# A fused two-layer graph attention on one core: step 1's first hidden tile turned by VectorE and sixteen transfers instead of TensorE

## The chip, the core and the metric

The kernel runs on one core of a Trainium2 chip. The metric is the device time of one execution in microseconds (us). The kernel before took 3073.7 us (median of three runs, 3072.74 to 3074.0).

Six instruction streams matter here. TensorE (PE; its weight loads are listed apart as PEld) multiplies and can also transpose a 128x128 tile. VectorE (DVE), ScalarE (ACT) and GpSimd (POOL) do the elementwise work. SyncE (SP) issues nearly all the transfers (DMA). Each stream runs its instructions in order, so an instruction that waits holds up whatever stands behind it on its own stream.

## What is computed

The input x is 64 graphs of 256 nodes with 512 features; adj is a boolean 256x256 adjacency per graph. Two layers are applied, each to a normalised and rectified copy of x, and each is added back:

```python
# layer 0
h = jnp.maximum(_layernorm(x, axis=-1), 0.0)
x = x + _L0_gnn_ref(h, adj, ...)      # 4 heads of 64, masked softmax attention over the 256 nodes, then Wo, bo
# layer 1
h = jnp.maximum(_layernorm(x, axis=-1), 0.0)
x = x + _L1_gnn_ref(h, adj, ...)      # layernorm with gamma, beta; 8 heads of 64; mask with the diagonal added; then w_out, b_out
```

All tiles are float32, apart from the masks.

## The kernel before

Two graphs form a step (G = 2, so 512 rows, in four row tiles t = 0 to 3 of 128 rows), and there are 32 steps. The steps are software-pipelined: while TensorE works on layer 1 of step s, the other engines prepare layer 0 of steps s+1 and s+2. The order of the work is written out by hand. Each call `at(period, place, function, ...)` puts a function at a place on a line of abstract time; at the end all calls are sorted by place and run, and this emits the instructions. Inside one engine they stay in that order. "Place" is therefore an order, not a time.

The matrix products use a seven-product scheme on 2x2 blocks (`PRODUCT`, the tuples `SET`, `SETC`), for which GpSimd builds sums of the weights (`weight_sum`, L410) and of the activations (`act_sums0`, `act_sums1`, L413 to L418). `project_qk` (L902) computes the queries and keys this way; its first product of a set needs only the block B0 of the turned activations `hT`, and its second (product 6) needs a sum, B4.

A product needs h with the features on the partitions, which is `hT`. There are two ways to get there:

- By TensorE. `transpose_h` (L735) does 16 transposes into PSUM, and ScalarE rectifies them out of PSUM into `hT` (L739). The function `by_tensor` says for which step and layer this is done: step 0 and, for layer 0, step 1, and for layer 1 the last step.
- By VectorE and transfers. `turn_blocks` (L759) transposes the 32x32 blocks of one row tile; `move_blocks` (L771) then carries the blocks to their partitions with sixteen transfers of 64 KB from SP; `place_h` (L782) rectifies them into `hT` on ScalarE. All the other steps do it so.

Step 0 has nothing to hide behind, so its front is special. `norm0` computes a row tile's mean and variance on VectorE (L647, L648, L676) and the inverse root on GpSimd (L677); `first_scale` (L688 on VectorE, L689 on ScalarE) scales it; `first_turn` (L798) transposes it on TensorE; `first_fill` rectifies the first graph (g = 0) and the second (g = 1) into `hT`, the even feature chunks on ScalarE (L809) and the odd on VectorE (L807); `first_qk` (L820) projects. For step 1 `norm0` computes all four tiles and `row_scales` (L657 to L659, GpSimd) and `scale_row` (L663, ScalarE) follow.

All early loads stand on SP's queue in this order: x of step 0 and Wq, Wk, Wv in halves, x of step 1 (L512), two of the eight transfers of w_qkv's first two blocks (L481), the adjacency of step 1 (L517), the other six, w_out (L478), Wo in two halves (L453), the two biases (L458), the third block of w_qkv, and later x of step 0 once more for the residual (`load_x`, L524). The program's list of waits has eight semaphores for SP's transfers, used in turn, so that each transfer also waits until the one eight places before it has landed.

The weights of layer 1 are turned on the way: `weight_turn` (L490) on VectorE for w_qkv, `weight_block` (L498 on TensorE, L500 out of PSUM on ScalarE) for w_out. `mask_scores` (L1078) adds the mask on VectorE, `exponentials` (L1083) are on ScalarE, `weigh` (L1126) multiplies with the values, `weigh_out` (L1141) copies the result out, `normalise` (L1202, GpSimd) divides by the sums, and for step 0 `combine_rows` (L1025) applies Wo.

Two limits of memory matter as well: PSUM has four banks for scores and four for everything else, and a product that takes a bank waits for the copy that empties it.

Of the kernel before, what the change touches and what calls it, by code (L numbers as in the profile page):

```python
# [8 lines left out]
FP = mybir.dt.float32  # L9
# [3 lines left out]
AF = mybir.ActivationFunctionType  # L13
# [305 lines left out]
def fast_path(  # L319
# [21 lines left out]
    nc = tc.nc  # L341
    P = 128
    B, N, D = x.shape
    DH = 64
    G = 2
    NSTEP = B // G
    NIC = N // P
    NT = G * NIC
    T = G * N
    NC = D // P  # L350
# [7 lines left out]
    act = ctx.enter_context(tc.tile_pool(name="act", bufs=1))  # L358
# [40 lines left out]
    Q, NQ = 32, P // 32  # L399
# [12 lines left out]
    def act_sums0(b, eng=nc.gpsimd):  # L412
        eng.tensor_tensor(b[:, 3], b[:, 5], b[:, 0], ALU.subtract)  # L413

    def act_sums1(b, eng=nc.gpsimd):
        eng.tensor_tensor(b[:, 4], b[:, 2], b[:, 3], ALU.subtract)
        eng.tensor_tensor(b[:, 5], b[:, 2], b[:, 5], ALU.subtract)
        eng.tensor_tensor(b[:, 6], b[:, 1], b[:, 4], ALU.subtract)  # L418


    H0, H1, HD = I0 // 2, I1 // 2, D // 2
# [3 lines left out]
    wo0 = const.tile([P, NB, HP0, HD], FP, name="wo0")  # L425
# [23 lines left out]
            )  # L449

    def later_weights():
        for i in range(2):
            nc.sync.dma_start(  # L453
                wo0[:, 2 * i:2 * i + 2].rearrange("p j c o -> p (j c) o"),
                wo[:, i * HD:(i + 1) * HD].rearrange("(c p) o -> p c o", p=P),
            )
        for v, t in ((bo, bo_b), (b_out, bout_b)):
            nc.sync.dma_start(t, bass.AP(tensor=v.tensor, offset=v.offset, ap=[[0, P], [1, D]]))  # L458

# [13 lines left out]
    def weight_load(n):  # L473

        pool, tag = ((act, "v1"), (io, "xt"), (act, "v1"), (act, "turned"))[n]
        wr = pool.tile([P, 4, D], FP, name="wr", tag=tag)
        if n == 3:
            nc.sync.dma_start(wr, w_out.rearrange("(r p) i -> p r i", p=P))  # L478
        else:
            for b in range(NQ):  # L480
                nc.sync.dma_start(  # L481
                    wr[b * Q:(b + 1) * Q].rearrange("p r i -> p (r i)").rearrange("p (r i) -> p r i", i=P),
                    w_qkv[n * D:(n + 1) * D, b * P:(b + 1) * P].rearrange("(r p) i -> p r i", p=Q),
                )
        return wr
# [199 lines left out]
    def first_scale(t):  # L685
        st = S[0]
        r, mr = st["r"][:, t:t + 1], st["mr"][:, t:t + 1]
        nc.vector.tensor_scalar(mr, st["mean"][:, t, 0:1], r, -1.0, op0=ALU.mult, op1=ALU.mult)  # L688
        nc.scalar.activation(st["h"][:, t, :], st["h"][:, t, :], AF.Identity, bias=mr, scale=r)  # L689

# [55 lines left out]

    def by_tensor(s, lyr):

        return s == 0 or s == (1, NSTEP - 1)[lyr]


    def turn_blocks(s, lyr, t):

        st = S[s]
        if "blocks" not in st:
            st["blocks"] = act.tile([P, NQ, NC, NT, Q], FP, name="blocks", tag=("turned", "h")[lyr])
        nc.vector.transpose(  # L759
            st["blocks"][:, :, :, t, :].rearrange("p b c n -> p c b n"),  # L760
            st["h"][:, t, :].rearrange("p (c b n) -> p c b n", c=NC, b=NQ),
        )
# [39 lines left out]
    def first_fill(g):  # L802
        for c in range(NC):
            b0, _, step = B_OF[c // HC]
            dst, src = S[0]["hT"][:, b0 + g * step, c % HC, :], S[0]["ph"][c][:, g]
            if c % 2:
                nc.vector.tensor_scalar(dst, src, 0.0, None, op0=ALU.max)  # L807
            else:
                nc.scalar.activation(dst, src, AF.Relu)  # L809

    def first_qk(g, i):

        st = S[0]
        if g == 0:
            st["qk", 0, i] = sm.tile([P, 2, T], FP, name="qk", bufs=2)
        bank = mm_tile([P, 2, N])
        terms = [(k, j, c) for k in range(2) for j in range(2) for c in range(HC)]
        for k, j, c in terms:
            b0, _, step = B_OF[j]
            nc.tensor.matmul(  # L820
                bank[:, k, :], wqk0[:, A_OF[i, j], c, k, :], st["hT"][:, b0 + g * step, c, :],
                start=(k, j, c) == terms[0], stop=(k, j, c) == terms[-1], skip_group_check=True,
            )

        def rest():
            cols = slice(g * N, (g + 1) * N)
            nc.vector.tensor_tensor(st["qk", 0, i][:, 0, cols], bank[:, 0, :], st["ne"][:, cols], ALU.mult)
            nc.scalar.copy(st["qk", 0, i][:, 1, cols], bank[:, 1, :])
        return rest
# [382 lines left out]
    def at(period, place, fn, *args):  # L1212
        events.append((period * (PERIOD if period >= 0 else FIRST) + place, len(events), fn, args))
# [7 lines left out]
    def at_set(period, place, order, fn, *args):  # L1221
        for i, n in enumerate(order):
            at_dense(period, place + i / 7, 1 / 7, fn, *args, n)
# [58 lines left out]
    AT_X, AT_C0, AT_QK, AT_Q0, AT_V0, AT_H1, AT_Z = 2.0, 3.0, 3.5, 4.5, 5.5, 6.06, 6.2  # L1282
# [8 lines left out]
    p = NSTEP - 2  # L1291
# [15 lines left out]
    for s in range(NSTEP):  # L1307

        p = s - 2
# [8 lines left out]
        else:  # L1318
            at(p - 1, 4.9, adjacency_pack, s)
        for t in range(NT):  # L1320
            at(p, ((0.5, 0.9, 1.73, 1.74)[t], (1.6995, 1.6996, 2.0295, 2.0296)[t], -6.3 + 0.01 * t)[s] if s < 3 else (0.95, 1.05, 1.2, 1.35)[t], norm0, s, t)
            if s == 0:
                at(p, (0.95, 1.35, 1.745, 2.15)[t], first_scale, t)
            else:
                at(p, (2.375 + 0.001 * t, (-5.8, -5.799, -5.6, -5.599)[t])[s - 1] if s < 3 else 1.6 + 0.001 * t, scale_row, s, t)
            if not by_tensor(s, 0):
                at(p, AT_X - 0.00035 + 0.00001 * t if s > 2 else (2.6, 2.601, 2.72, 2.721)[t], turn_blocks, s, 0, t)
        if not by_tensor(s, 0):
            at(p, AT_X - 0.00031 if s > 2 else 3.0, move_blocks, s)
        for g in range(G):  # L1330
            if s < 3:
                at(p, (1.8, 2.03, -5.8)[s] + 0.001 * g, neighbours, s, g)
            else:
                at(p - 1, AT_Q0 - 0.0009, neighbours, s, g)
        if s < 2:
# [5 lines left out]
        for a in range(NQ if s > 2 else 0):  # L1341
            place = AT_X - 0.00031 if a > 2 else 1 + (a + 4) / 7 - 0.0005
# [4 lines left out]
        if s == 0:  # L1347
            at(p - 1, 5.72, warm)
            for t in range(NT):
                at(p, (1.0, 1.4, 3.31, 3.32)[t], first_turn, t)  # L1350
            for g in range(G):
                at(p, (1.72, 3.33)[g], first_fill, g)
                for i in range(2):
                    rest = []
                    place, end = ((3.0, 3.5), (3.64, 3.969), (3.97, 4.299), (4.3, 4.638))[g * 2 + i]
                    at(p, place, lambda g=g, i=i, rest=rest: rest.append(first_qk(g, i)))
                    at(p, end, lambda rest=rest: rest[0]())
        else:
            for c in range(NC):
                if by_tensor(s, 0):  # L1360
                    at(p, 2.9292 + 0.0001 * c, transpose_h, s, 0, c)
                else:
                    at(p, AT_Q0 - 0.001 + 0.0001 * c, place_h, s, 0, c)
            at(p, AT_Q0 - 0.0005 if s > 1 else FIRST_C0 + 0.1, lambda s=s: act_sums0(S[s]["hT"]))
            at(p, AT_Q0 - 0.0004 if s > 1 else FIRST_C0 + 0.101, lambda s=s: act_sums1(S[s]["hT"]))
            at_set(p, 3.3 if s < 2 else AT_Q0, SET, project_qk, s, 0, 0)
        if s < 2:
            for t in range(NT):
                place = (FIRST_V0 + 0.14 * t - (0 if t else 0.0005), (4.31, 5.02, 5.16, 5.31)[t])[s]
# [7 lines left out]
        p = s - 1  # L1377
# [20 lines left out]
        for k in range(NT):  # L1398
# [6 lines left out]
            place = ((3.6112, 3.6113, 3.7502, 3.7503)[k], 3.6 + 0.01 * k, AT_Q0 + (-0.0002, -0.00019, 0.0002, 0.00021)[k])[edge]  # L1405
# [11 lines left out]
        p = s  # L1417
        if s < NSTEP - 1:
# [3 lines left out]
            p, place = (s + 1, 1.0) if s < NSTEP - 2 else (s, LAST_QK + 2)  # L1422
# [5 lines left out]
        else:  # L1428
            p = s - 1
# [43 lines left out]
    gbr, blocks = [], {}  # L1473
    at(-3, 5.7, first_loads)
    at(-3, 5.705, lambda: gbr.append(first_gamma()))
    at(-2, 4.93, later_weights)
    for i in range(4):
        at(-2, 4.301 if i else FIRST_Q0 + 0.32, weight_sum, nc.gpsimd, wqk0, i)
        at(-1, 1.21, weight_sum, nc.gpsimd, wo0, i)
    for n, place in ((0, 4.0), (1, 4.0), (3, 4.0), (2, 5.0)):  # L1480
        at(-2, place, lambda n=n: blocks.update({n: weight_load(n)}))
    at(-2, FIRST_V0 + 0.2, lambda: gamma_beta(gbr[0]))
    for i in range(12):
        place = (
            4.6395, 4.6396, 4.9, 4.901, 4.902, 5.19965, 5.19966, 5.7, 12.6, 12.601, 12.602, 13.0,
        )[i]
# [55 lines left out]
```

## Time and profile before

| | |
|---|---|
| median of three runs | 3073.7 us (3072.74 to 3074.0) |
| the profiled execution: its time, and the span of its profile | 3072.65 us, 3070.9 us |
| busy, of the span: PE, DVE, POOL, ACT | 3063.4, 2534.3, 2295.8, 1212.2 us |
| PE busy from 15 to 3000 us | 2984.96 of 2985 us |
| granted TensorE clock | 1.00 up to 3000 us, 0.98 in the last 71 us |
| DMA share in 5 to 10, 15 to 20, 20 to 25, 30 to 35, 50 to 55 us | 1.12, 1.26, 1.23, 0.89, 0.16 |
| the 16 transposes of step 1 for layer 0 (L735) on the chain of waits | 34.27 us, for 1.75 us |

A timeline row has the start in us from the start of the span, the time it covers, the engine (SPq and ACTq are transfers being issued), the line, the operation, the tile written and the tiles read, the shape, and in square brackets the idle time in front of it with what ended it. In a view of groups, the last numbers are busy time and the mean of one in ns. The DMA share is the mean busy share of the 16 DMA engines; packets that wait in a queue count, so it can pass 1.

### The profile page before, as it was taken

The page shows a single profiled execution, that of the slowest core. Times are in us where ns is not written, and L with a number is a line of the kernel's source. Part 1 is how long each engine was busy: PE and PEld are TensorE (multiplying, and loading weights), DVE is VectorE, ACT ScalarE, POOL GpSimd, SP SyncE. Part 2 cuts the span into 40 slices and gives each one's busy share as a digit, 9 for nine tenths or more (in the row PEclk, how much of TensorE's full clock was granted, in tenths as well). Part 3 has the DMA queues.
Part 4 walks back from the last instruction along what each step waited for, and adds up shares of the span by engine and source line. Part 5 has one row for each costly group of instructions (what it writes and reads, how often), then busy time and mean ns, then how long its engine had stood idle before and what let it go on. Part 6 is the DMA issues. An engine that isn't in the chain of part 4 may idle for free.

```text
span 3070.9 us, 55407 instructions
## 1 busy us (share of the span) xinstructions
PE 3063.4 (100%) x20106; PEld 2527.4 (82%) x20106; DVE 2534.3 (83%) x4739; ACT 1212.2 (39%) x2133; POOL 2295.8 (75%) x2120
## 2 busy tenths in 40 slices
PE   9999999999999999999999999999999999999999
PEld 7888888888888888888888888888888888888887
DVE  7888888888888888888888888888888888888766
ACT  5443443434343343433444333443434344343431
POOL 6877787777877777777877777787777877778753
PEclk9999999999999999999999999999999999999999
DMA  6223222233222331323323233222232222332311
GB/s 159 58 88 95 78 75 85 74 95 95 60 88 71 100 95 53 91 73 94 95 60 90 74 89 94 75 77 80 81 94 83 72 83 74 101 91 56 92 35 50
DMA packets 192365, 251.20 MB, mean 82 GB/s; under 512 B 58264, under 2 KB 84504, under 8 KB 192088
## 3 DMA queue, kind: packets, MB, share of 16 engines
q1 hardware_dynamic: 128800, 180.46, 20.8%
q10 hardware_dynamic: 63288, 67.15, 7.5%
q8 instruction: 161, 2.64, 0.4%
q14 instruction: 116, 0.95, 0.1%
HBM read 128.59 MB, written 34.34 MB: 53 GB/s over the span
## 4 chain that ended last, share of the span: by engine, by line
PE 100%; DVE 0%; issue 0%; ACT 0%; POOL 0%; POOLq 0%
PE mm L902 38%; PE mm L999 19%; PE mm L983 13%; PE sc L1055 9%; PE sc L1126 6%; PE mm L949 6%; PE mm L1126 5%; PE mm L1055 3%; PE mm L932 1%; PE mm L1025 0%; PE mm L820 0%; PE mm L789 0%; PE mm L735 0%; PE mm L498 0%; PE sc L798 0%; PE mm L553 0%
## 5 line engine op out<-in xcount | busy, mean ns | idle before, releaser
L902 PE MATMUL mm<-hT,wqkv 128*128 128x256 f32 x3584 | 787.4, 380 | 0.0
L902 PEld LDWEIGHTS mm<-hT,wqkv 128*128 128x128 f32 x3584 | 677.9, 190 | 102.6 <-issue 11.4
L1090 POOL TENSOR_TENSOR pd<-p 128x512 f32<-128x512 f32 x383 | 480.1, 1275 | 253.4 <-ACT p L1083 195.5
L999 PE MATMUL mm<-wo,oT 128*128 128x256 f32 x2632 | 578.8, 379 | 0.0
L999 PEld LDWEIGHTS mm<-wo,oT 128*128 128x128 f32 x2632 | 499.7, 190 | 69.2 <-issue 0.7
L1083 ACT ACTIVATE p<-p 128x512 f32<-128x512 f32 x766 | 441.4, 627 | 102.8 <-DVE p L1078 91.1
L1078 DVE TENSOR_TENSOR p<-sc,n 128x512 f32<-128x512 f32 x579 | 363.1, 683 | 113.1 <-PE sc L1055 113.1
L983 PE MATMUL mm<-wqkv,hT 128*128 128x256 f32 x1792 | 395.2, 381 | 0.0
L902 PE MATMUL mm<-hT,wqk 128*128 128x256 f32 x1736 | 383.7, 381 | 0.0
L983 PEld LDWEIGHTS mm<-wqkv,hT 128*128 128x128 f32 x1792 | 337.9, 190 | 55.0 <-issue 10.3
L902 PEld LDWEIGHTS mm<-hT,wqk 128*128 128x128 f32 x1736 | 327.0, 190 | 53.5 <-issue 10.3
L870 POOL TENSOR_TENSOR xt<-xt,u 128x512 f32<-128x512 f32 x183 | 233.1, 1274 | 140.3 <-DVE xt L864 67.4
L1055 PE MATMUL sc<-qk 64*128 64x256 f32 x2320 | 292.7, 385 | 0.0
L1055 PEld LDWEIGHTS sc<-qk 64*128 64x128 f32 x2320 | 217.8, 186 | 59.7 <-issue 27.6
L1096 DVE STREAM_TRANSPOSE turned_p<-pd 128x1024 f32<-128x1024 f32 x192 | 237.2, 1235 | 26.6 <-POOL pd L1090 25.9
L663 ACT ACTIVATE h<-h,mr,r 128x512 f32<-128x512 f32 x252 | 187.9, 806 | 170.0 <-POOL mr L659 170.0
L1202 POOL TENSOR_TENSOR oT<-oT 128x512 f32<-128x512 f32 x188 | 240.2, 1278 | 1.1 <-DMA oT<-line 1.1
L1103 DVE TENSOR_REDUCE part<-turned_p 128x32 f32<-128x1024 f32 x192 | 233.2, 1215 | 4.4
L1126 PE MATMUL sc<-p,v 128*32 128x256 f32 x3152 | 190.8, 382 | 0.0
L949 PE MATMUL mm<-hT,wv 128*128 128x256 f32 x840 | 188.3, 382 | 0.0
L855 ACT COPY u<-mm 128x512 f32<-128x512 f32 x62 | 36.4, 586 | 368.9 <-PE mm L999 221.7
L949 PEld LDWEIGHTS mm<-hT,wv 128*128 128x128 f32 x840 | 156.6, 190 | 26.8 <-ACT vT L836 6.2
(162 smaller groups left out, 4443.9 us busy)
## 6 DMA issues: line engine op xcount, KB each, us to landing
h<-blocks SPq DMA_DIRECT2D x960, 64.0 KB, 2.0
oT<-line SPq DMA_DIRECT2D x376, 128.0 KB, 3.0
h<-in_x_dram SPq DMA_DIRECT2D x31, 1024.0 KB, 5.6
xt<-in_x_dram ACTq DMA_DIRECT2D x60, 512.0 KB, 4.8
out_dram<-xt SPq DMA_DIRECT2D x32, 512.0 KB, 3.1
v<-values ACTq DMA_DIRECT2D x480, 32.0 KB, 1.9
out_dram<-xt ACTq DMA_DIRECT2D x30, 512.0 KB, 4.4
ne<-ne SPq DMA_DIRECT2D x90, 64.0 KB, 2.0
```

Source lines behind the costliest of these rows:

```text
L902: nc.tensor.matmul(bank[:, k, :], w[:, wa, c, k, a * P:(a + 1) * P], st["hT"][:, ba, c, :], start=first and (k, c) == (0, 0), stop=(k, c) ...
L949: nc.tensor.matmul(bank, wv0[:, wa, c, :], st["hT"][:, ba, c, :], start=first and c == 0, stop=c == HC - 1, skip_group_check=True,)
L983: nc.tensor.matmul(bank[:, t, :], st["hT"][:, ba, c, t * P:(t + 1) * P], wqkv1[:, wa, c, 2, :], start=first and (t, c) == (0, 0), stop=(t, ...
L999: nc.tensor.matmul(bank[:, t, :], oT[:, ba, c, t * P:(t + 1) * P], w[:, wa, c, :], start=first and (t, c) == (0, 0), stop=(t, c) == (NIC - ...
L1055: nc.tensor.matmul(sc[g][e][:, kc, :], qk[rows, 1, k0:k0 + P], qk[rows, 0, g * N:(g + 1) * N], start=True, stop=True,)
L1078: nc.vector.tensor_tensor(p[e][:, g], sc[e], neg[:, :, g, :], ALU.add)
L1083: nc.scalar.activation(p[e][:, g], p[e][:, g], AF.Exp, scale=SCALE)
L1090: nc.gpsimd.tensor_tensor(st["pd"][:, e], p[e][:, :, 0, :], p[e][:, :, 1, :], ALU.add)
L1096: nc.vector.transpose(st["turned_p"], st.pop("pd").rearrange("p e g (b k) -> p (e g b) k", k=32))
L1103: nc.vector.tensor_reduce(st["part", lyr, prs][:, i], st.pop("turned_p"), axis=mybir.AxisListType.X, op=ALU.add)
L1126: nc.tensor.matmul(po[r0:r0 + 32, g, :], (st["v1"][:, g * NIC + kc, pr * P + r0:pr * P + r0 + Q] if lyr else st["v0"][:, r0 // Q, pr, g * ...
L1202: nc.gpsimd.tensor_tensor(dst, dst, invb, ALU.mult)
```

## The change

Six things change, all in the first 50 us of the program. From there on the order of each engine's work is the same as before.

1. `by_tensor` no longer holds for step 1 of layer 0: its `transpose_h` is replaced by `turn_blocks`, `move_blocks` and `place_h`. The `blocks` tile takes the buffer with the tag "h".
2. `norm0` of step 1 moves up in front of the second and third result of `first_qk` on VectorE, `row_scales` on GpSimd in front of the masks of step 0, and `scale_row` on ScalarE in front of the third copy of `first_qk`. The neighbour maxima of step 1 (`neighbours`, L587) move behind the turns.
3. `first_fill` of graph 0 is done by ScalarE alone, and VectorE does the odd chunks of graph 1 only.
4. `first_scale` of row tile 1 is cut into two halves of 256 columns; for row tile 3 its VectorE part moves in between the two neighbour maxima of step 0.
5. The load of w_out moves in front of w_qkv's first block on SP's queue.
6. Wo is loaded by one transfer instead of two.

On SP's queue the sixteen new transfers stand behind the eight of w_qkv and in front of Wo, the two biases, the third block of w_qkv, the first line of sums (L1173) and `load_x`. The buffers change with the order: `load_x` of step 0 now takes the buffer that holds w_qkv's second block until its last `weight_turn`, where it took the buffer of step 1's h before; and the last of the four score banks of step 0's second pair of heads is one that `mask_scores` has to empty first, where it was one that `weigh_out` had to empty.

```diff
     def later_weights():
-        for i in range(2):
-            nc.sync.dma_start(
-                wo0[:, 2 * i:2 * i + 2].rearrange("p j c o -> p (j c) o"),
-                wo[:, i * HD:(i + 1) * HD].rearrange("(c p) o -> p c o", p=P),
-            )
+        nc.sync.dma_start(
+            wo0[:, :4].rearrange("p (i j) c o -> p i (j c) o", i=2), wo.rearrange("(c p) (i o) -> p i c o", p=P, i=2)
+        )
...
-        nc.scalar.activation(st["h"][:, t, :], st["h"][:, t, :], AF.Identity, bias=mr, scale=r)
+        for cols in (slice(0, D // 2), slice(D // 2, D)) if t == 1 else (slice(0, D),):
+            nc.scalar.activation(st["h"][:, t, cols], st["h"][:, t, cols], AF.Identity, bias=mr, scale=r)
...
-        return s == 0 or s == (1, NSTEP - 1)[lyr]
+        return s == 0 or (s, lyr) == (NSTEP - 1, 1)
...
-            st["blocks"] = act.tile([P, NQ, NC, NT, Q], FP, name="blocks", tag=("turned", "h")[lyr])
+            st["blocks"] = act.tile([P, NQ, NC, NT, Q], FP, name="blocks", tag="h" if lyr or s == 1 else "turned")
...
-            if c % 2:
+            if g and c % 2:
                 nc.vector.tensor_scalar(dst, src, 0.0, None, op0=ALU.max)
...
-            at(p, ((0.5, 0.9, 1.73, 1.74)[t], (1.6995, 1.6996, 2.0295, 2.0296)[t], -6.3 + 0.01 * t)[s] if s < 3 else (0.95, 1.05, 1.2, 1.35)[t], norm0, s, t)
+            at(p, ((0.5, 0.9, 1.73, 1.74)[t], 1.231 + 0.001 * t, -6.3 + 0.01 * t)[s] if s < 3 else (0.95, 1.05, 1.2, 1.35)[t], norm0, s, t)
             if s == 0:
-                at(p, (0.95, 1.35, 1.745, 2.15)[t], first_scale, t)
+                at(p, (0.95, 1.35, 1.745, 1.80005)[t], first_scale, t)
             else:
-                at(p, (2.375 + 0.001 * t, (-5.8, -5.799, -5.6, -5.599)[t])[s - 1] if s < 3 else 1.6 + 0.001 * t, scale_row, s, t)
+                at(p, (1.7 + 0.001 * t, (-5.8, -5.799, -5.6, -5.599)[t])[s - 1] if s < 3 else 1.6 + 0.001 * t, scale_row, s, t)
             if not by_tensor(s, 0):
-                at(p, AT_X - 0.00035 + 0.00001 * t if s > 2 else (2.6, 2.601, 2.72, 2.721)[t], turn_blocks, s, 0, t)
+                at(p, AT_X - 0.00035 + 0.00001 * t if s > 2 else 2.0295 + 0.0001 * t if s == 1 else (2.6, 2.601, 2.72, 2.721)[t], turn_blocks, s, 0, t)
         if not by_tensor(s, 0):
-            at(p, AT_X - 0.00031 if s > 2 else 3.0, move_blocks, s)
+            at(p, AT_X - 0.00031 if s > 2 else (2.03, 3.0)[s - 1], move_blocks, s)
         for g in range(G):
             if s < 3:
-                at(p, (1.8, 2.03, -5.8)[s] + 0.001 * g, neighbours, s, g)
+                at(p, (1.8, 2.3685, -5.8)[s] + 0.0001 * g, neighbours, s, g)
...
-                    at(p, AT_Q0 - 0.001 + 0.0001 * c, place_h, s, 0, c)
+                    at(p, (AT_Q0 - 0.001 if s > 1 else 2.9292) + 0.0001 * c, place_h, s, 0, c)
...
-    for n, place in ((0, 4.0), (1, 4.0), (3, 4.0), (2, 5.0)):
+    for n, place in ((3, 3.1), (0, 4.0), (1, 4.0), (2, 5.0)):
         at(-2, place, lambda n=n: blocks.update({n: weight_load(n)}))
```

## The prediction

> **What bounds the kernel now.** I read the page first, then the chain of waits of the first 62 us, then that stretch's timeline with the DMA issues, because the change touches nothing later.
>
> ```profile
> span 3070.9 us, 55407 instructions
> PE 3063.4 (100%) x20106; PEld 2527.4 (82%) x20106; DVE 2534.3 (83%) x4739; ACT 1212.2 (39%) x2133; POOL 2295.8 (75%) x2120
> ```
>
> TensorE works all the time. Work taken from it is therefore gained in full, and every new stop of it is lost in full: with PE busy 2984.96 of 2985 us from 15 us on, there is no idle time later that could swallow either. At most 7.5 us of idle exist, 1.39 at the start (for the identity) and most of the rest in the last 71 us. The chain around the transposes:
>
> ```profile
> 30.62 3.65 PE mm L932 x16
> 34.27 1.75 PE mm L735 x16
> 36.02 1.86 PE sc L1126 x32
> 37.88 1.93 PE sc L1055 x16
> 39.81 1.92 PE mm L902 x8
> 41.73 0.44 PE mm L498 x4
> ```
>
> The 16 transposes take 1.75 us, and TensorE does not stop in front of them or behind them. What stands on the other engines at that moment:
>
> ```profile
> 34.74 2.07 ACT L739 ACTIVATE hT<-mm 128x512 f32<-128x512 f32 x4
> 37.51 1.28 DVE L490 STREAM_TRANSPOSE wqkv<-wr 128x512 f32<-128x512 f32 x2
> 37.95 0.59 ACT L1141 COPY oT<-sc 128x512 f32<-128x512 f32 x1 [1.14 <-PE sc L1126]
> 38.43 1.28 ACT L612 ACTIVATE rows<-identb,any_of 128x128 bf16<-128x128 bf16 x4
> 38.98 2.48 DVE L1078 TENSOR_TENSOR p<-sc,n 128x512 f32<-128x512 f32 x4 [0.19 <-PE sc L1055]
> 39.70 2.43 ACT L1083 ACTIVATE p<-p 128x512 f32<-128x512 f32 x4
> 42.50 0.65 ACT L500 COPY wo<-mm 128x256 f32<-128x256 f32 x2
> 44.18 0.61 PE L498 MATMUL mm<-ident,wr 128*128 128x128 f32 x4
> ```
>
> ScalarE has 1.14 us of idle here and VectorE 0.19. Neither has much in reserve if something comes late. The last row is TensorE's second `weight_block`; it needs the bank that the ACT copies at 42.50 empty, and it stands 1.03 us behind them. And the transfers:
>
> ```profile
> 12.74 8.54 SPq L481 DMA_DIRECT2D wr<-in_L_gnn_w_qkv_dram  x6
> 21.33 1.26 SPq L478 DMA_DIRECT2D wr<-in_L_gnn_w_out_dram  x1
> 141.44 10.03 SPq L771 DMA_DIRECT2D h<-blocks  x16
> wr<-in_L_gnn_w_out_dram SPq DMA_DIRECT2D x1, 1024.0 KB, 10.1
> h<-blocks SPq DMA_DIRECT2D x960, 64.0 KB, 2.0
> ```
>
> With a DMA share over 1 from 5 to 30 us, the early loads keep all engines of the queue full; the last of the set (w_out) lands at 21.33 + 10.1 = 31.4 us.
>
> **The change, part by part.**
>
> *Front of graph 0.* ScalarE fills four chunks at 0.33 us (two took 0.66) instead of two, from 7.78: 8.11, 8.44, 8.77, 9.10. `first_qk` needs chunk c 0.46 us after chunk c-1 (eight products in 3.7 us), so the odd ones come in time. VectorE saves 0.76 us at 7.89, but h of tile 2 lands only at 3.23 + 5.2 = 8.4, so the statistics start at 8.45, not 8.56. The halves of tile 1 cost ScalarE 2 x about 0.5 us (an estimate between 0.33 for 256 columns out of PSUM and 0.81 for 512) instead of 0.81, while the first transposes may start at 7.38 instead of 7.42: -0.15 to +0.2 us. GpSimd's chain of root, cast (1.04) and rows (1.45) moves with the statistics by 0.1 us, and TensorE's neighbour products wait for it, so the 0.62 us stop at 12.4 changes place more than size. Sum: -0.1 us, bounds -0.8 and +0.2. As TensorE stops at 40 us for what does not depend on this (below), I count 0.
>
> *Statistics and scaling of step 1 moved up.* h of step 1 lands at 6.92 + 9.3 = 16.2. Four tiles at 0.82 us end at 19.5; GpSimd's `row_scales` follows (23.51 to 25.65 before: 2.15 us) until 21.65; ScalarE scales four rows in 2.94 us until 24.6; VectorE's four turns at 0.67 us run behind and end at 25.35. Queued behind them: on GpSimd the masks (16.98 before) wait until 21.4 and end near 25, needed at 27.8; then the sums of weights (5.1 us) and the cast (1.04) fill it to 31.1, so the key halves start 0.5 us later than 30.63. On VectorE the fourth result, the maxima (1.27) and two weight turns (1.29) end at 28.35, so `mask_scores` starts 0.54 us later than 27.81. On ScalarE the third copy (21.93) moves to 24.6; its scores come at 26.5. All of this is hidden by TensorE's own 34 us of work, but it leaves VectorE 0.54 us late at 38.98, which is the place where its reserve is 0.19.
>
> *Loads.* w_out in front only changes the order within the set: after h (16.2) come w_out (31.4 - 28.8 = 2.6), the adjacency (0.7) and eight loads of w_qkv (24.1, 25.6, 27.2 and 28.8 from issue plus landing: 1.55 each), so the last w_qkv lands near 31.4 - 31.9. One issue of Wo saved is 0.6 us of SP at a time when nothing waits for SP: 0.
>
> *Sixteen transfers.* They could start at 25.35. But by the program's list of waits transfer k waits for the one eight before; the eighth waits for the last w_qkv load, at 31.4. From there eight more issues at 10.03 / 16 = 0.63 us: the sixteenth goes at 36.4 and lands 2.0 later, at 38.4. Lower bound, if that wait did not bind: 25.35 + 15 x 0.63 + 2.0 = 36.8. Upper bound, with the slowest steady set (11.85 / 16 = 0.74) and a landing of 3.8 us, as the last transfers of the set at 110 us have: 31.4 + 5.9 + 3.8 = 41.1. I take 38.4, since the eight semaphores are in the program. Before, `hT` was begun at 34.74.
>
> The Trainium skill speaks against such transfers: "DMA: Bandwidth & Descriptors", section "Bandwidth", has 0.95 us for 64 KB by itself and calls transfers below 64 KB dominated by their descriptors. By its figure the last eight would need 7.6 us instead of 5.0, and the loss below would be 2.6 us larger. The row of this case (0.63 us) is what I use.
>
> *What the late `hT` costs.* ScalarE stands at `place_h` until 38.4. Four at 0.616 us (L782 in later steps) end at 40.86. Behind it, in order, is what ran from 37.95 to 43.15 before: the output copy, the rows, four exponentials, the copy of product 1, two copies of w_out: 5.2 us. It ends at 46.06. TensorE's second `weight_block` waits for that; it began at 44.18 before. **Loss: 1.9 us.** On the way there TensorE has time to spare: without the transposes it is through `weigh` at 36.0, then the last score bank waits for `mask_scores` (38.98 + 0.54 + 0.68 = 40.2, a stop of about 3 us in all), the rest of the scores takes 0.72, product 1 1.92, the first block 0.44: 43.3; product 6 (1.73, its sum B4 is ready at 42.3) and the adjacency's transposes (0.45) bring it to 45.5. So even with the transfers in time VectorE's chain alone would put that block at 45.5, 1.3 us later than before. The 1.75 us removed are contained in this, since TensorE only waits longer.
>
> *What is late next.* `load_x` waits for the last turn of w_qkv's second block, which follows `mask_scores`: 42.0 + 0.7 = 42.7 instead of 37.81, landing 5.9 later at 48.6. GpSimd's bias then starts at 48.6 instead of 44.53, and its chain (4.97, 1.27, 2.29, about 2, 1.27 us) brings the second `normalise` to an end at 60.6 instead of 56.94. `combine_rows` began at 58.84; with 1.9 us of delay TensorE reaches it at 60.7. It just holds. Everything on GpSimd after that stands 2.14 us idle at 67.45 and catches up.
>
> **Sum.** +1.9 us on the profiled execution's 3072.65, 3074.55. The median of the runs is 1.05 us above that execution, so I predict **3075.6 us**.
>
> **The rivals.**
>
> *Gain as meant.* The transfers land before 34.3, and VectorE's mask is in time; then the 1.75 us and up to 0.5 of the front come off: 3073.7 - 2.0 = 3071.7. For it: ScalarE waits 1.14 us at 37.95, so a little lateness is free. Against it: the lower bound of 36.8. Chance 0.12.
>
> *Mask alone.* The eight semaphores do not bind and the transfers land at 36.8; ScalarE ends at 44.5, TensorE's block comes at 45.5 through VectorE: +1.3, 3075.0. If VectorE is also 0.5 us earlier than I think and the front gives 0.5, about zero, 3074. Chance 0.2.
>
> *Slower beyond 0.2%.* The sixteen are issued among the weight loads at those loads' own pace, 8.54 / 6 = 1.42 us, and land with a delay of 8 as theirs do: 31.4 + 8 x 1.42 + 8 = 50.8, ScalarE's chain ends at 58.4, 14 us late; with the landing of 2.0 it is 8.3 us, 3082. It decides from a landing at 42.7. Against it: in my order nothing but the sixteen is on the queue by then, and Wo and the biases come behind. Chance 0.11.
>
> TensorE's clock is no rival by the rows: the stop of 0.62 us at 12.4 left it at 1.00. "TensorE: Matmul & The Clock Gate", section "What's actually happening", halves it after an idle window of some 3.4 us; my longest stop is 3 us, and if it were tripped, a further 1.7 us would be an estimate by that page.
>
> **How the numbers follow.** My forecast (late by 1 to 4 us, 3074.7 to 3078) has 0.57, the rivals 0.12, 0.2 and 0.11. A measurement of this kernel tells about 0.2%, 6.1 us, from no change. The range reaches from 3073.0, which leaves out the gain, to 3080.0, which takes in the upper bound of 41.1 (+4.6) and the lower edge of the third rival: some 0.8 is inside. No case gives a gain of 6 us, since there is no such time to be had; slower by 6 us is the third rival and little else.
>
> **What would show it.** L735 gone from step 1 and sixteen L771 issues between 25 and 39 us, the last landing near 38.4; `place_h` on ScalarE ended by that DMA; TensorE idle at L1055 near 37 to 40 us until L1078, and again near 45.5 in front of L498; L537 starting near 48.6; all rows after 60 us shifted by about 1.9. I am wrong if `place_h` starts before 36 us, if the eighth transfer does not wait for the last w_qkv load, or if TensorE has no idle between 34 and 47 us.

## The result, and the profile after

The kernel after took 3082.74 us (median of eight runs, 3081.57 to 3083.98), the kernel before on the same chip 3072.93 us (eight runs, 3072.2 to 3074.05). The ratio is 1.0031, with a 95% interval of 1.002 to 1.0042. The forecast was 3075.6 with a range of 3073.0 to 3080.0, from a loss of 1.9 us: the loss had the forecast sign and was about five times as large (9.8 us). The profiled execution after took 3083.98 us, the longest of its eight.

The head of the page, after:

```profile
span 3082.2 us, 55406 instructions
PE 3067.6 (100%) x20090; PEld 2529.0 (82%) x20090; DVE 2535.9 (82%) x4741; ACT 1211.3 (39%) x2136; POOL 2296.2 (74%) x2120
```

The span is 11.3 us longer. VectorE and GpSimd did the same amount of work as before; a total cannot show where 11 us went. A landmark does: a group of 56 products of one shape (L983 before, L982 after) that TensorE runs at about 100 us, behind all the changed work. Its row in the timeline of before, and of after:

```profile
97.98 12.35 PE L983 MATMUL mm<-wqkv,hT 128*128 128x256 f32 x56
```

```profile
109.49 12.35 PE L982 MATMUL mm<-wqkv,hT 128*128 128x256 f32 x56
```

They start 11.51 us later and take the same 12.35. The whole loss lies in front of them. Line numbers after are one or two lower than before (L901 after is L902 before): L901 are the products of `project_qk`, L837, L839 and L841 the additions by which VectorE empties their results out of PSUM, L1054 the scores, L1077 the mask. Where TensorE stopped there (the list of its waits from 30 to 100 us, after: total, times, longest):

```profile
PE mm L901 <- DVE qk L841: 4.1, 1, 4.1
PE sc L1054 <- DVE p L1077: 2.2, 1, 2.2
PE mm L901 <- DVE qk L839: 1.3, 1, 1.3
```

Before, this list is empty. The 2.2 us are the stop that was forecast. The other 5.4 us were not. What happened at the forecast stop, from the timeline after:

```profile
38.85 2.19 ACT L781 ACTIVATE hT<-h 128x512 f32<-128x512 f32 x4 [4.05 <-DMA h<-blocks]
...
39.97 1.13 PE L1054 MATMUL sc<-qk 64*128 64x256 f32 x6 [2.23 <-DVE p L1077]
...
41.03 3.12 PE L901 MATMUL mm<-hT,wqk 128*128 128x256 f32 x8
```

The sixteen transfers landed at 38.85, the mask came at 39.97. Then eight products took 3.12 us where the same shape took 1.92 before. The windows of one microsecond say why (length, busy time of PE, PEld, DVE, ACT and POOL with instructions, then granted clock, DMA share, GB/s):

```profile
42.00:43.00 1.00, 1.00 (x4) 0.82 (x3) 1.00 (x3) 1.00 (x4) 1.00 (x2) 0.50 0.55 181
...
44.00:45.00 1.00, 1.00 (x6) 1.00 (x5) 0.00 (x0) 1.00 (x3) 1.00 (x2) 0.50 1.14 224
```

The clock stood at half for 3.42 us, from 41.7 to 45.2 (the shares below 1.00, added up): 1.7 us more. The two unforeseen stops begin in SP's queue. First the issues of before (start, length, what is issued), then those of after:

```profile
32.06 2.06 SPq L481 DMA_DIRECT2D wr<-in_L_gnn_w_qkv_dram  x4
37.37 0.33 SPq L1173 DMA_DIRECT2D line<-keys  x1
...
40.80 1.15 SPq L1184 DMA_DIRECT2D oT<-line  x2
42.00 0.58 SPq L512 DMA_DIRECT2D h<-in_x_dram  x1
```

```profile
37.40 0.74 SPq L452 DMA_DIRECT2D wo<-in_L_gnn_Wo_dram  x1
...
39.39 2.79 SPq L479 DMA_DIRECT2D wr<-in_L_gnn_w_qkv_dram  x4
42.28 3.94 SPq L1172 DMA_DIRECT2D line<-keys  x1
...
52.51 1.14 SPq L1183 DMA_DIRECT2D oT<-line  x2
53.75 0.54 SPq L510 DMA_DIRECT2D h<-in_x_dram  x1
```

SP spent 25.64 to 37.35 us on the sixteen transfers. So Wo, the two biases and the third block of w_qkv (0.5 + 0.5 + 1 MB), which were out by 34.12 before, went out between 37.40 and 42.18. The line of sums, 4 KB, stands behind these 2 MB. It went out 4.9 us later than before. Its issue and its landing, in the list of transfers after (KB, us from issue to landing):

```profile
line<-keys SPq DMA_DIRECT2D x1, 4.0 KB, 10.2
```

Before, it had landed at the latest when the transfer that reads it was issued, at 40.80, 3.4 us after its issue. After, this took until 52.5. Both stops follow from it in the timeline:

```profile
52.57 1.25 DVE L1095 STREAM_TRANSPOSE turned_p<-pd 128x1024 f32<-128x1024 f32 x1 [4.90 <-DMA line<-keys]
...
59.67 0.69 DVE L645 BATCH_NORM_STATS2 bs<-h 128x6 f32<-128x512 f32 x1 [2.11 <-DMA h<-in_x_dram]
```

VectorE's sums of the second pair of heads (L1095) wait until the line of the first pair has landed; before (L1096) they began at 44.62 and waited for nothing. L839, which TensorE needs, stands behind them (56.89, where its counterpart ran at 48.93 before): 1.3 us. Step 2's h is issued on SP behind the copies out of that line (L1183), at 53.75 instead of 42.00; VectorE's four statistics of it stand in front of L841, which comes at 62.88 instead of 53.35: 4.1 us, and a second stretch of half clock, 6.82 us long. The rows before, the row after, and the ten microseconds with the second stretch, after:

```profile
44.62 1.24 DVE L1096 STREAM_TRANSPOSE turned_p<-pd 128x1024 f32<-128x1024 f32 x1
...
53.35 0.69 DVE L842 TENSOR_TENSOR qk<-mm,qk 128x512 f32<-128x512 f32 x1 [0.55 <-PE mm L902]
```

```profile
62.88 0.66 DVE L841 TENSOR_TENSOR qk<-mm,qk 128x512 f32<-128x512 f32 x1
```

```profile
60.00:70.00 10.00, 6.32 (x23) 5.16 (x24) 7.82 (x16) 2.67 (x3) 9.47 (x11) 0.66 0.10 29
```

Stops of 2.2 + 1.3 + 4.1 us; 1.7 us of the first half-clock stretch, and 2.7 of the second (0.34 of 60 to 70 us, less the 0.7 in which TensorE stood anyway); less the 1.3 by which the change with free transfers is in front of before (experiment three, below): 10.7 of the 11.5.

### The profile page after: what moved, and what is told of

Same layout as the page of the kernel before. It is cut to its first block, busy times and chain, and to the rows that moved or that the text cites. A ratio compares the mean times of both kernels' runs of the same rounds, so it can differ in the third digit from the quotient of the medians.

```text
span 3082.2 us, 55406 instructions
## 1 busy us (share of the span) xinstructions
PE 3067.6 (100%) x20090; PEld 2529.0 (82%) x20090; DVE 2535.9 (82%) x4741; ACT 1211.3 (39%) x2136; POOL 2296.2 (74%) x2120
## 4 chain that ended last, share of the span: by engine, by line
PE 98%; DMA 1%; DVE 1%; SPq 0%; issue 0%; POOL 0%; ACT 0%; DVEq 0%
PE mm L901 38%; PE mm L998 18%; PE mm L982 13%; PE sc L1054 9%; PE mm L948 6%; PE sc L1125 6%; PE mm L1125 5%; PE mm L1054 3%; PE mm L1024 0%; DMA h<-in_x_dram 0%; DMA wr<-in_L_gnn_w_qkv_dram 0%; PE mm L931 0%; DVE p L1077 0%; DVE bs L645 0%; PE mm L734 0%
## 5 line engine op out<-in xcount | busy, mean ns | idle before, releaser
L901 PE MATMUL mm<-hT,wqkv 128*128 128x256 f32 x3584 | 787.4, 380 | 0.0
L901 PEld LDWEIGHTS mm<-hT,wqkv 128*128 128x128 f32 x3584 | 678.0, 190 | 102.5 <-issue 11.4
L1077 DVE TENSOR_TENSOR p<-sc,n 128x512 f32<-128x512 f32 x579 | 362.7, 681 | 110.9 <-PE sc L1054 110.9
L982 PE MATMUL mm<-wqkv,hT 128*128 128x256 f32 x1792 | 395.2, 381 | 0.0
L901 PE MATMUL mm<-hT,wqk 128*128 128x256 f32 x1736 | 387.3, 383 | 5.4 <-DVE qk L841 4.1
L982 PEld LDWEIGHTS mm<-wqkv,hT 128*128 128x128 f32 x1792 | 337.8, 190 | 55.1 <-issue 10.3
L901 PEld LDWEIGHTS mm<-hT,wqk 128*128 128x128 f32 x1736 | 328.7, 191 | 60.2 <-issue 10.3
L1054 PE MATMUL sc<-qk 64*128 64x256 f32 x2320 | 293.3, 385 | 2.2 <-DVE p L1077 2.2
L1054 PEld LDWEIGHTS sc<-qk 64*128 64x128 f32 x2320 | 217.9, 186 | 62.5 <-issue 27.2
L1095 DVE STREAM_TRANSPOSE turned_p<-pd 128x1024 f32<-128x1024 f32 x192 | 237.1, 1235 | 35.4 <-POOL pd L1089 29.5
```

Of the source, the lines that this page charges most:

```text
L901: nc.tensor.matmul(bank[:, k, :], w[:, wa, c, k, a * P:(a + 1) * P], st["hT"][:, ba, c, :], start=first and (k, c) == (0, 0), stop=(k, c) ...
L982: nc.tensor.matmul(bank[:, t, :], st["hT"][:, ba, c, t * P:(t + 1) * P], wqkv1[:, wa, c, 2, :], start=first and (t, c) == (0, 0), stop=(t, ...
L1054: nc.tensor.matmul(sc[g][e][:, kc, :], qk[rows, 1, k0:k0 + P], qk[rows, 0, g * N:(g + 1) * N], start=True, stop=True,)
L1077: nc.vector.tensor_tensor(p[e][:, g], sc[e], neg[:, :, g, :], ALU.add)
L1095: nc.vector.transpose(st["turned_p"], st.pop("pd").rearrange("p e g (b k) -> p (e g b) k", k=32))
```

## The experiments

Two theories. Theory Q: the loss is the queue, since the sixteen transfers push the line of sums and step 2's h back. Theory L: a late `hT` shifts what is behind it, whatever the queue holds. Beside the times I give the landmark, the start of the 56 products, in each one's profiled execution. That is one execution: in seven it took 3086.02 us, 3.1 above the median, and in six 3074.4, 2.5 under it, so between kernels the medians count and the landmark shows where the time went. The table's first column names each by its number; the medians have 4 to 10 runs, and the kernel before took 3072.83 to 3073.06 us beside them.

| kernel | median us | ratio, interval | landmark, against 97.98 |
|---|---|---|---|
| after | 3082.74 | 1.0031 (1.002 to 1.0042) | +11.51 |
| 1 third block behind step 2's h | 3079.07 | 1.002 (1.001 to 1.0029) | +6.27 |
| 2 TensorE turns | 3071.86 | 0.9997 (0.9988 to 1.0007) | -0.43 |
| 3 no transfers | 3071.39 | 0.9995 (0.9986 to 1.0005) | -1.28 |
| 4 as 1, masks first | 3078.84 | 1.0019 (1.001 to 1.0029) | +6.94 |
| 5 third block behind both lines | 3077.82 | 1.0014 (1.0005 to 1.0024) | +3.12 |
| 6 as 5, masks first | 3076.89 | 1.0013 (1.0003 to 1.0022) | +1.14 |
| 7 TensorE turns, transfers aside | 3082.92 | 1.0033 (1.0019 to 1.0048) | +13.85 |
| 8 turning alone | 3086.79 | 1.0043 (1.0026 to 1.0059) | +12.85 |
| 9 as 7, third block behind both lines | 3074.09 | 1.0007 (0.9998 to 1.0017) | +1.41 |

### One: the third block of w_qkv behind step 2's h

```diff
-    for n, place in ((3, 3.1), (0, 4.0), (1, 4.0), (2, 5.0)):
+    for n, place in ((3, 3.1), (0, 4.0), (1, 4.0), (2, 5.36)):
```

> Edit: on SP's queue the third block of w_qkv (four loads of 256 KB) goes behind h and adjacency of step 2 instead of in front of the first line of sums. Queue theory (the line of sums and h of step 2 land late because, behind the sixteen transfers, they stand behind 2 MB of weights; TensorE's stops of 1.3 and 4.1 us at 57 and 60 us and the lowered clock after them follow from that): the line lands within 4 us of its issue instead of 10.2, both stops go, and about 8.8 us come back: 3073 to 3075.5. Mask theory (the stop of 2.2 us in front of the scores at 40 us is the root and the later ones only follow): 3080 or more. Turn theory (VectorE's added work is the price): 3080 or more.

It took 3079.07 us: 3.7 us better than after, and not the 3073 to 3075.5 expected. The first line now went out at 38.33 and landed within 5.3 us, and the stops at 57 and 60 us fell from 5.4 us to 0.5. But there is a second line, of the second pair of heads, and the block now stood in front of that one. The issues, and what waited for them:

```profile
45.99 5.11 SPq L479 DMA_DIRECT2D wr<-in_L_gnn_w_qkv_dram  x4
51.22 0.88 SPq L1172 DMA_DIRECT2D line<-keys  x1
...
62.84 1.26 POOL L1201 TENSOR_TENSOR oT<-oT 128x512 f32<-128x512 f32 x1 [3.72 <-DMA oT<-line]
```

GpSimd stands idle for 3.72 us before it divides by the sums, and TensorE's Wo (L1024) waited 3.2 us for it. The stop moved along the queue with the block: for theory Q, against my choice of place.

### Two and three: the turn by TensorE again, and the turn by VectorE without transfers

Two keeps the five other edits and restores one line; three keeps VectorE's turns and lets ScalarE read them in place.

```diff
-        return s == 0 or (s, lyr) == (NSTEP - 1, 1)
+        return s == 0 or s == (1, NSTEP - 1)[lyr]
```

> Edit: step 1's h of layer 0 is turned by TensorE again; all other parts of the change stay (early statistics and scaling, ScalarE's fill, halves, w_out in front, Wo in one load). Queue theory and mask theory both: no stop from 35 to 70 us, 3072 to 3074. If one of the other parts carries the loss: 3076 or more.

```diff
     def move_blocks(s):
...
         blocks = st.pop("blocks")
...
+        if s == 1 and "hT" not in st:
+            st["moved"] = blocks.rearrange("p b c t n -> p (b c t n)").rearrange("p (a c t n) -> p a c t n", a=NQ, c=NC, t=NT)
+            return
```

> Edit: the changed kernel without the sixteen transfers; ScalarE reads VectorE's turned blocks as they are, so the 32x32 blocks of step 1's layer 0 stay on the wrong partitions and its attention is computed from those. VectorE's turns, the order and all other instructions stay. Queue theory: the stops at 57 and 60 us go, that at 40 us (2.2 us and the lowered clock) stays, the 1.75 us of transposes are gained: 3072.5 to 3075. Mask theory: 3079 or more. Turn theory: 3080 or more.

3071.86 and 3071.39 us, 0.1 and 1.1 under the intervals expected, and both inside what the measurement cannot tell from before. The five other edits cost nothing that can be told here, and neither do VectorE's turns. All of the loss hangs on the transfers. Three also has a miss: I expected the stop at the mask to stay, and TensorE does not stop there at all: its sixteen scores run from 35.81 in 2.36 us (2.00 in two), and the one stop left, 0.2 us, is for VectorE's L840 at 43.5. Why the mask no longer holds TensorE is not shown. And three shows about what the turn could have brought in this order of work: without its transposes, its landmark is 0.85 us in front of two's, and 0.5 us in the median.

### Four: the masks in front as well

The kernel of one, with two turns of w_qkv's second block (`weight_turn` i = 5 and 6 on VectorE, 1.28 us) moved so that `mask_scores` comes first.

```diff
-            4.6395, 4.6396, 4.9, 4.901, 4.902, 5.19965, 5.19966, 5.7, 12.6, 12.601, 12.602, 13.0,
+            4.6395, 4.6396, 4.9, 4.901, 4.902, 5.6998, 5.6999, 5.7, 12.6, 12.601, 12.602, 13.0,
```

> Edit: as e1_third_block_late, and two of VectorE's turns of w_qkv's second block (1.28 us) go behind the masks of step 0's second pair. Queue theory: the stop at 40 us shrinks from 2.2 to about 1 us, the clock stays at 1.00 there, and 1.5 to 2.5 us come off e1's time: 3071 to 3073.5. Mask theory: this one recovers most where e1 does not, 3073 to 3076. If ScalarE's late chain sets the restart and not the mask: no more than 0.5 us under e1.

3078.84 us, a miss: the wait for the mask fell from 1.7 to 0.6 us, and 0.2 us came of it. TensorE stood later instead: 2.1 us for GpSimd, whose second line is still behind the block, and 2.5 for L841, where one has 0.5. That second stop is not only TensorE coming sooner; L841 itself ran at 56.91, in one at 55.15, because VectorE waited for step 2's h:

```profile
53.70 0.69 DVE L645 BATCH_NORM_STATS2 bs<-h 128x6 f32<-128x512 f32 x1 [1.91 <-DMA h<-in_x_dram]
```

This h went out at 43.68, 1.2 us sooner than in one, and landed 10.0 us after its issue, where one has 6.6. Both profiles have the block's loads 1.1 us behind h; why it took longer here is not shown. So four does not tell what the mask alone is worth.

### Five and six: the third block behind both lines

```diff
-    for n, place in ((3, 3.1), (0, 4.0), (1, 4.0), (2, 5.0)):
+    for n, place in ((3, 3.1), (0, 4.0), (1, 4.0), (2, 5.88)):
```

Six has this and the masks of four. (What the expectation of six calls two mask turns are the same two turns of w_qkv's second block; they go behind the masks.) In the traces of both the first of the block's four loads still went out in front of the second line (45.29 against 50.93 in five); the other three stand behind it.

> The changed kernel with one place altered: the third block of w_qkv is issued behind both lines of sums and behind both halves of step 2's inverse degrees, so nothing that graph 0's front needs stands behind it. hT is still as late as the sixteen transfers make it. Theory Q (the loss is the queue: line of sums and h of step 2 behind 2 MB of weights): the stops at 57 to 64 us of TensorE go, the clock is 0.95 or more from 45 to 70 us, what stays is the wait for the mask, 1.7 to 2.2 us, and less than 1 us behind it, less the 1.75 us of transposes: 3073 to 3075.5. Theory L (a late hT alone shifts everything behind it, whatever the queue holds): 3078 or more, with stops over 2 us behind 50 us.

> The kernel of e5_third_block_last with step 1's two mask turns of the second row tile taken from VectorE's late place and put ahead of the scores of the last pair. If the wait for the mask is a real part of the rest it falls under 1 us and the time is 0.5 to 1.5 us under e5's: 3072 to 3074. If what ends the scores is not the mask but the lateness of its weights, no difference to e5 within 0.3 us.

Five took 3077.82 us, 2.3 above what theory Q gave it, though its waits are those expected (TensorE, 30 to 100 us):

```profile
PE sc L1054 <- DVE p L1077: 1.8, 1, 1.8
PE mm L901 <- DVE qk L841: 0.8, 1, 0.8
```

What I had not counted is in the windows:

```profile
40.00:45.00 5.00, 5.00 (x21) 3.73 (x19) 2.70 (x4) 4.36 (x12) 5.00 (x4) 0.71 0.54 147
```

After a stop of 1.8 us the clock was halved from 39.5 to 42.9 us; it is granted at 0.95 from 35 to 40 us and at 0.71 here, and costs 0.05 x 5 + 0.29 x 5 = 1.7 us. The landmark adds up: 1.8 + 0.8 + 1.7, less the 1.3 by which three's landmark is in front of before's, is 3.0, and 3.12 was measured. Six has stops of 1.0, 0.6 and 0.5 us and no lowered clock in its profile; its landmark is +1.14. Its median, 3076.89, is 0.9 us under five's, as expected, and above the 3072 to 3074 named; but the two sets of times overlap (five 3075.56 to 3078.53), so the 0.9 is not shown, and six's ten times lie in two groups (three from 3074.4 to 3075.09, seven from 3076.49 to 3079.89). Two more executions of it were profiled.

> The kernel of e6_third_last_masks_first once more, for its profile: its ten times lay in two groups, 3074.4 to 3075.1 and 3076.5 to 3079.9, and the profile was of the lowest. If the clock makes the groups, a profile of 3076.5 or more has the same stops within 0.5 us as that one and a stretch of some 3.4 us at a granted clock of 0.5, which is 1.7 us. If a stop makes them, the profile has a longer one, 2 us or more, with the clock at 1.00.

> As e6_again_a, a second look at the same kernel, since one look may fall in the lower group again.

One took 3076.53 us, the other 3074.2. The clock was 1.00 in both up to 100 us, so it does not part these two; the stops do, as the second answer named, though the longest is 1.7 us and not 2. The waits of the longer one:

```profile
PE mm L901 <- DVE qk L841: 1.7, 1, 1.7
PE mm L901 <- POOL hT L416: 0.7, 1, 0.7
...
```

and of the shorter one:

```profile
...
PE mm L901 <- DVE qk L841: 0.5, 1, 0.5
```

The stops left out are alike (0.6 to 0.7 us). The longer ones go with later transfers: in the longer execution the sixteen were issued from 24.84 to 36.84 and landed for `place_h` at 38.34; in the shorter one from 24.32 to 35.93, landing at 37.42. That is 0.9 us at `place_h` and 2.3 us in the time; two executions do not show that the one makes the other. Whether the executions near 3079 have a stretch of half clock, no profile shows.

### Seven and nine: the queue filled, `hT` early

TensorE turns h as in two, and SP issues sixteen transfers of the same size at the same place that copy h to a tile that no engine reads. Nine also has five's edit, the third block behind both lines.

```diff
+    def copy_aside():
...
+        st = S[1]
+        aside = act.tile([P, NQ, NC, NT, Q], FP, name="blocks", tag="h")
+        h = st["h"].rearrange("p t d -> p (t d)").rearrange("p (a c t n) -> p a c t n", a=NQ, c=NC, t=NT)
+        for a in range(NQ):
+            for b in range(NQ):
+                nc.sync.dma_start(aside[b * Q:(b + 1) * Q, a], h[a * Q:(a + 1) * Q, b])
...
+            at(p, 2.03, copy_aside)
```

> The changed kernel with step 1's h turned by TensorE as before, and sixteen transfers of 64 KB still issued by SP at the same place, which copy step 1's h to a tile that no engine reads; so SP's queue is as full as in the changed kernel and hT is as early as before. Theory Q: the line of sums and h of step 2 are issued as late as in the changed kernel (42 and 53 us, 5 us or more later than before), stops at 57 to 64 us of 4 us or more and a lowered clock behind them: 3078 to 3082. Theory L: nothing waits for the copies, 3072 to 3073.5.

> The kernel of e7_transfers_aside (step 1's h turned by TensorE, sixteen transfers to a tile that no engine reads) with the third block of w_qkv behind both lines of sums and behind both halves of step 2's inverse degrees. Theory Q: with the queue mended nothing is left to lose, since hT is early: no stop over 1 us behind 30 us, clock 0.97 or more there, 3071.5 to 3074, that is 9 to 11 us under e7_transfers_aside. If SP's sixteen issues cost by themselves, whatever stands behind them: over 3077.

Seven took 3082.92 us, 0.9 above the interval expected: with `hT` as early as before (begun at 34.80, before 34.74) and no engine reading the copies, the loss is all there. Its waits from 38 to 66 us:

```profile
DVE turned_p L1104 <- DMA line<-keys: 9.8, 1, 9.8
...
PE mm L910 <- DVE qk L848: 6.3, 1, 6.3
```

and its issues:

```profile
43.24 2.99 SPq L1181 DMA_DIRECT2D line<-keys  x1
...
54.53 1.14 SPq L1192 DMA_DIRECT2D oT<-line  x2
55.72 0.58 SPq L510 DMA_DIRECT2D h<-in_x_dram  x1
```

TensorE gets to the same two waits without the stop at 40 us, and in this profile stands at them for 6.3 and then 2.9 us. (The second is put down to GpSimd's L678, which ended at 66.20; VectorE's L850, the counterpart of L841, ended at 66.19.) Theory Q is shown and L falls as the cause of the whole. Nine, 3074.09 us, is 8.8 us under seven with one number changed, 0.1 above the interval expected. Its issues, and the one stop that is left and that I had said would not be there:

```profile
39.32 0.37 SPq L1181 DMA_DIRECT2D line<-keys  x1
...
45.66 0.58 SPq L510 DMA_DIRECT2D h<-in_x_dram  x1
```

```profile
PE mm L910 <- POOL n L630: 1.9, 1, 1.9
```

The profile names GpSimd's mask (L630, ended at 56.12) as the last in front of this product, which reads `hT` and weights; L850 ended at 56.07, and it stood behind the four statistics of step 2's h, for which VectorE had waited 2.6 us. This h goes out at 45.66, not 42.00, since SP is busy with the sixteen until 36.2 us and has Wo and the biases behind them. So the stop is most likely the second one of after, made short, and most of the 2.2 us above two: what is left of a full queue. No run separates a transfer's place in the queue from its sharing the transfer engines with the loads in front of it.

So four kernels make a square. `hT` early: 3071.86 with the queue free (two) and 3082.92 with it full (seven). Third block out of the way: 3074.09 with `hT` early (nine) and 3077.82 with it late (five). In the kernel after, both are late, and it takes 3082.74: no more than seven. The late `hT` costs 3.7 us when the queue is mended, and nothing when it is not: TensorE then waits in that time for what the line holds up (6.3 us in seven).

### Eight: the turning alone

Edits 3 to 6 of the change are undone, the earlier statistics stay: the fill shared with VectorE, tile 1 scaled whole, tile 3 scaled at its old place, w_out behind w_qkv, Wo in two loads.

```diff
-            if g and c % 2:
+            if c % 2:
...
-                at(p, (0.95, 1.35, 1.745, 1.80005)[t], first_scale, t)
+                at(p, (0.95, 1.35, 1.745, 2.15)[t], first_scale, t)
...
-    for n, place in ((3, 3.1), (0, 4.0), (1, 4.0), (2, 5.0)):
+    for n, place in ((0, 4.0), (1, 4.0), (3, 4.0), (2, 5.0)):
```

> Only the turning by VectorE with its sixteen transfers and the earlier statistics; the fill shared with VectorE, the second tile scaled whole, w_out behind w_qkv and Wo in two loads as before the change. If the turning carries the whole loss: 3081 to 3084, with the same stops at 40, 57 and 60 us. If the small edits (less work for VectorE, fewer issues on SP or the other way round, an added load ahead) carry a part: 3078 or less.

3086.79 us (four runs): 4 us worse than after, where I expected 3081 to 3084 or less. Here the sixteen are issued from 24.74 to 38.58, and `place_h` starts at 40.09; the line goes out at 44.22 and what reads it at 54.83, each some 2 us later than after. After, with w_out in front of w_qkv and one issue of Wo fewer, the sixteen were through 1.2 us sooner. Without the transfers the small edits are worth no more than can be told (two), and with the queue full some 4 us; which of them, I did not try.

## Why the prediction was wrong, step by step

*Front of graph 0, counted 0.* It held: two is 1.0 us under before, inside its interval. The landmark gives -0.43, within the bounds of -0.8 and +0.2.

*Statistics, scaling, turns.* Statistics from 15.92 to 19.1 (forecast 16.2 to 19.5), turns to 24.94 (25.35). They cost nothing, as three shows.

*The sixteen transfers.* Forecast: the sixteenth issued at 36.4, `place_h` at 38.4. It was 36.76 and 38.85. The eighth was issued at 31.77 (31.4), and SP had waited 1.3 us in all for w_qkv's loads. The set took 11.7 us, 0.73 each with that wait in it, and the last one 0.59, near the row of 0.63 that I took. The Trainium skill's page "DMA: Bandwidth & Descriptors", section "Bandwidth", has 0.95 us for 64 KB, measured on loads from HBM that GpSimd issued; for these transfers, from SP and between partitions, it would have been too much as a pace.

*What the late `hT` costs, +1.9.* The first half held: the mask came at 39.97 (forecast 40.2), TensorE stood for 2.2 us (about 3), ScalarE's copies ended at 45.78 (46.06). But the second `weight_block` began at 47.15, not 46.06, 3.0 us later than before, and TensorE did not wait for ScalarE there: the list of its waits has no such stop. I had given TensorE's own way to that block 45.5; half a clock for 3.42 us, 1.7 us, makes 47.2 of it. So what set the block was TensorE itself. Up to here the forecast was 1.1 us short, and the clock accounts for that.

*The clock.* I wrote that it was no rival, from a stop of 0.62 us, which says nothing of one of 2 or 3. The runs have half clock after stops of 2.2 and 4.1 us (after), 2.5 (four), 3.2 (one), 3.9 (eight), 6.3 (seven), and once after 1.8 (five); none after 2.1 (four at 66 us), 1.9 (eight at 38 us, nine) and 1.7 (one at 38 us, the longer execution of six); those of 2.9 (seven) and 2.3 (eight) fell into a stretch that had begun. The Trainium skill's page "TensorE: Matmul & The Clock Gate", section "What's actually happening", lets the clock fall after an idle window of some 3.4 us; stops well below it were enough here, so as a limit for a single stop the figure does not hold. As a length it does: each stretch measured here is a multiple of 3.41 us within 0.02, and the price of 1.7 us was right.

*What is late next: the step that failed.* I followed one transfer behind the sixteen, `load_x`, and let the rest of the queue be. (Even that one went out at 46.32, not 42.7, as SP stood at the line's issue, and GpSimd's bias, L535 after, began at 55.02, not 48.6.) My own list named Wo, the biases, the third block and the line of sums as standing behind them. What I did not do was to date the line: 2 MB of loads that had been out of the way by 34.12 us now went out immediately in front of a 4 KB transfer, and step 2's h came behind both. The line was read at 52.5, not 40.8; h was issued at 53.75, not 42.00. "It just holds" was said of GpSimd's chain (whose terms, from 48.6, add up to 60.4 and not 60.6, which decides nothing), and the chain that broke was VectorE's, two waits in front of TensorE. At 47 us the loss was 3.0 us, at the landmark 11.5: this step left out 8.5. The runs give the same size: 8.8 us between seven and nine, where `hT` is early and the third block is all that differs. With `hT` late, between after and five, it is 4.9 us in the medians (8.4 at the landmark of the two profiled executions).

*The rivals.* The third rival named 3082 and a queue, but another one: there the sixteen themselves landed at 42.7 or later. They landed at 38.85; the queue behind them was the trouble, so that its number is nearly the measured one is luck. The gain as meant was to bring 2.0 us, 1.75 of them from the transposes; three, where the transfers are free, has 0.5 us against two, where TensorE still does them, so this rival had little to win. The mask alone (3074 to 3075) had the right end, 3076.1 for five without its 1.7 us of clock, in a queue that was not that of the change.

*What would show me wrong.* None of the three signs appeared (`place_h` before 36 us, the eighth transfer not waiting, no idle of TensorE between 34 and 47 us), and the number was wrong all the same. They tested the part that I had worked out, and none of them looked at a row behind it. Of the signs for the forecast, TensorE's idle time in front of the block near 45.5 did not come. The row that would have shown it is the last one I gave: everything after 60 us shifted by 1.9 us. It was 11.5.

## What to carry to other kernels

When a block of transfers is put into a queue, date every transfer behind it, the smallest first: here a line of 4 KB that an engine waits for paid for the megabytes in front of it. Loads that nothing needs for long belong behind the short transfers; putting 1 MB behind both lines (in five, all but its first quarter behind the second) was worth 4.9 us here with a late `hT` (five), and 8.8 us with an early one (nine). Two late chains beside each other cost here the longer of the two: mending `hT` alone brought nothing (seven), and with the queue mended 3.7 us.

## What had not been expected of the hardware

TensorE's clock is halved in whole portions. The shares below 1.00 add up to 3.42 us in after, 3.42 in one and in four, 3.40 in five; the second stretch of after has 6.82, that of eight 10.24, that of seven 13.64: one, two, three and four times 3.41. Near 2 us a stop may or may not set it off: 1.8 us did in five, 1.9 did not in eight and 2.1 did not in four. And it comes late, often when TensorE is working again (after: idle from 37.7 to 40.0, half clock from 41.7).

A short transfer took its time from what stood in front of it: the line of 4 KB landed 10.2 us after its issue behind 2 MB of weights, 4.6 us behind 1 MB (five), and 3.6 us with no load directly in front of it (two). Its issue itself took 3.94 us on SP in the first case and 0.33 to 0.37 in the others.
